# Layer 0's last turns: where the weighing's copies stand on ScalarE, and which PSUM tiles the last output chunks use

## The chip, the cores and the metric

The kernel runs on one core of a Trainium2 chip. The metric is the device time of one execution in microseconds (us), of which several are taken. A core has a matrix engine (TensorE, PE in the profile; its weight loads are a row of their own, PEld), a vector engine (VectorE, DVE), a scalar engine (ScalarE, ACT), GpSimd (POOL) and SyncE (SP), which here issues the DMAs. Each engine runs its own list of instructions in order, and they wait for one another through semaphores. All data is float32. Matrix products write to PSUM, which this kernel divides into eight banks of 128 partitions by 512 float32.

## The reference

The program is four residual layers on an image batch `x` of shape (2, 512, 64, 64): each layer normalises by groups of channels, computes a branch and adds it to `x`. The change lies in the first layer (attention over a 3x3 window and over pooled tokens at once, 8 heads of 64 channels) and at the first instructions of the second (attention with sampled keys). The first layer's branch, on the normalised tokens `xf` (N = 4096 pixels, C = 512), cut to what matters:

```python
q = (xf @ W_q + b_q).reshape(B, N, nh, hd).transpose(0, 2, 1, 3)
q_norm = _l2norm(q)
q_scaled = (q_norm + query_embedding[None]) * softplus(temperature)[None]
# k_local, v_local: the 9 shifted copies of normalised k, and of v
attn_local = jnp.einsum('bhnd,bhndk->bhnk', q_scaled, k_local)
# k_pool, v_pool: keys and values of 256 pooled tokens
attn_pool = jnp.einsum('bhnd,bhpd->bhnp', q_scaled, _l2norm(k_pool))
attn = softmax(concatenate([attn_local, attn_pool], axis=-1), axis=-1)
a_local, a_pool = (attn[..., :ll], attn[..., ll:])
lt = jnp.einsum('bhnd,hdk->bhnk', q_norm, learnable_tokens) + learnable_bias[None] + a_local
x_local = jnp.einsum('bhnk,bhndk->bhnd', lt, v_local)
x_pool = jnp.einsum('bhnp,bhpd->bhnd', a_pool, v_pool)
xo = (x_local + x_pool).transpose(0, 2, 1, 3).reshape(B, N, C)
out = (xo @ W_proj + b_proj).reshape(B, C, H, W)
```

The last line reshapes without a transpose, so a product of `xo` with `W_proj` gives rows of tokens that are added to the image in strides of eight (the `r` below). The second layer begins with the query `q = w_q x` of its normalised input, and with offsets of the sampled keys that come from a small network on strided pixels of that query.

## The kernel before

The two images of the batch are computed one after the other, so that everything here happens twice in an execution. The first layer (class `Local`) cuts an image into 16 units: four chunks of 128 channels times four quarters of 1024 pixels. A software pipeline of turns i = -4 to 16 runs over them (`run`, L2031 to L2060). In one turn several generators are stepped in rotation by `in_turn`: the normalisation and the projections of q, k and v for units three and four ahead, the products of unit i+1, the attention of unit i, the weighing of unit i-1.

- `learned` (L2412) computes the learnable part of the local weights: eight small products (L2419) and one activation (L2422), and then the scaled query (L2424).
- `tap_products` (L2436) copies a unit's query from SBUF to a query tile in PSUM, two halves (L2441, ACT), and DVE multiplies it by the nine shifted keys (L2447). `tap_sums` sums these products over the channels of a head on PE (L2474) into a tap bank.
- `attend` (L2486) takes the pooled scores (L2499, PE), exponentials (L2503, ACT), values (L2509, PE), their copy (L2511, ACT), the sums of the exponentials (L2525 and L2528, PE), the reciprocals on DVE, and sends the finished weights to DRAM (L2566).
- `weigh` (L2586) has ten steps for a unit. A DMA has spread a tap's row of weights over 64 partitions (L2584, from `rows`). ACT copies the tap's two halves to two PSUM banks (L2600). DVE multiplies them by the shifted values (L2608), or, in step 0, the unit's pooled output by the reciprocal sums (L2605). POOL adds the result to the unit's output (L2613). The next tap is fetched into the freed slot, of which there are three, or five for the last unit. The finished unit is stored to DRAM (L2619).
- `output` (L2211) multiplies the stored units by `W_proj`. `output(c4)` makes the image's channel chunk c4, in eight groups r of four products `product(ps, kc, r)` (L2227), one for each of the four chunks of contracted channels. `added` then runs three operations on DVE: the bias (L2231), the addition to the image (L2232) and the statistics for the next normalisation (L2233). After eight groups they are aggregated (L2303). `output(0)` runs in turn 14, `output(1)` in 15, `output(2)` in 16 and `output(3)` after the loop. Each reads the units through DRAM, but for `output(2)` and `output(3)` the unit of the last contracted chunk is read where the weighing leaves it (`late` in the profile).

The next layer's input is normalised by folding: from the statistics of a chunk come mean and reciprocal deviation (`part_stats`, `stats_in_steps`: PE L965, DVE L966 to L968, PE L970, ACT L971, DVE L972, POOL L973), `scale_part` (L978) scales the next layer's weights, and `thin` (L1208, ACT) copies strided pixels for the offsets.

The eight PSUM banks at this place are five of a ring (`bank()`, pool name `mm`), one tap bank (`tap`, pool `ppt`), and one query tile of two banks (`qs`, pool `pps`). A new tile in a place waits until the readers of the old one have ended. Two halves of one query tile are one tile in this accounting.

The order of PE's instructions is written by hand (`manual_schedule`) in the steady turns (3 to 11) and in turn 16. In turns 12 to 15 and in `output(3)` the scheduler of the framework orders them, as it orders the other engines everywhere. `issue_after(x)` tells it to place what stands inside behind the instruction x on their engine.

The second layer begins in `query_and_sample` (L1249): the offset network's first products go to four banks of the ring (L985), their sums to an accumulator `acc` of four banks (L992, L1006), which is read by L994 and L1009, then follow the activation of the offsets (L1223) and the query's first product (L134), whose result is read by L1264.

Of the kernel before, what the change touches and what calls it, by code (L numbers as in the profile page):

```python
# [9 lines left out]
F32 = mybir.dt.float32  # L10
# [6 lines left out]
P = 128  # L17
# [4 lines left out]
TB = 512  # L22
# [28 lines left out]
def in_turn(*gens):  # L51


    gens = list(gens)
    while gens:
        gens = [g for g in gens if next(g, gens) is not gens]
# [877 lines left out]
class Net(General):  # L934
# [314 lines left out]
    def query_and_sample(self, X, Y, wq, bq, grid, feats, top, wp, pp, ppk):  # L1249
# [9 lines left out]

        def query(blk):  # L1260
            for cc in range(KC):
                ps = pp.tile([P, TB], F32, name="mm")
                self.project(ps, wq[:, :, cc * P:(cc + 1) * P], X, blk)
                nc.scalar.activation(Y[:, cc, blk * TB:(blk + 1) * TB], ps, AF.Identity,  # L1264
                                     bias=bq[:, cc:cc + 1])
                yield
            nc.vector.tensor_reduce(top[:, :, blk], Y[:, :, blk * TB:(blk + 1) * TB], AX.X, ALU.max,
                                    apply_absolute_value=True)
# [673 lines left out]
class Local:  # L1942
# [77 lines left out]
    def run(self):  # L2020


        self.nmean = self.net.stats[:, 0]
        xs = self.pooled_tokens()
        heads = self.pooled_heads(xs)
        units = KC * self.UN
        unit = lambda u: u if 0 <= u < units else None
        self.pending = []
        for i in "qkv":
            self.fetch(i, 0)  # L2030
        for i in range(-4, units + 1):  # L2031
            k, q, ahead, u, before = (unit(i + n) for n in (4, 3, 1, 0, -1))
            self.steady = self.UN <= i + 1 and i < units - 4
            streams, ended = [], []
            stages = [self.norms(streams, ended)]
            if ahead is not None:
                stages.append(self.tap_products(ahead))
            if u is not None:
                stages.append(self.attend(u))
            if i == units:  # L2040
                stages.append(self.output(KC - 2))
            if before is not None:
                stages.append(self.weigh(before))
            if ahead is not None:
                stages.append(self.tap_sums(ahead))
            values = ([ahead] if i >= self.UN - 1 and ahead is not None
                      else {-4: [0], -3: [1, 2], -2: [3]}.get(i, []))
            stages.append(self.projections(k, q, values, streams))
            stages.append(self.normed(ended))
            if i < -2:  # L2050
                stages.append(islice(heads, 12 if i == -4 else None))
            if i == units - 3:
                stages.append(self.fetch_output())
            if units - 3 < i < units:
                stages.append(self.output(i - units + 2))
            if self.steady or i == units:
                with self.net.tc.manual_schedule(engines={mybir.EngineType.PE}):
                    in_turn(*stages)
            else:
                in_turn(*stages)  # L2060

        self.nc.sync.dma_start(self.next_w, self.d["w_q1"].rearrange("(kc p) o -> p kc o", p=P))
        in_turn(self.output(KC - 1))

# [144 lines left out]
    def output(self, c4):  # L2211
# [15 lines left out]
            nc.tensor.matmul(ps, toks[kc].rearrange("p (i r) -> p r i", r=8)[:, r, :], self.sq[kc],  # L2227
                             start=(kc == 0), stop=(kc == KC - 1))

        def added(ps, r):  # L2230
            nc.vector.tensor_tensor(ps, ps, self.pb, ALU.add)  # L2231
            nc.vector.tensor_tensor(xx[:, r], xx[:, r], ps, ALU.add)  # L2232
            nc.vector.bn_stats(st[:, r, :], xx[:, r])  # L2233

        def wide():
            qs = self.pps.tile([P, self.UT], F32, name="qs")
            return [qs[:, j * TB:(j + 1) * TB] for j in range(2)]

        def extras(r):
            if c4 and r == 2:  # L2240
                net.part_stats(slice(c4 - 1, c4), self.pp)
                net.thin(self.X, self.Y, c4 - 1)
            if c4 == KC - 1 and r:
                net.scale_part(self.next_w, slice(r // 2 - 1, r // 2))

        if c4 < KC - 2:
            yield
            yield
            for r in range(0, 8, 2):
                banks = [self.bank() for _ in range(2)]  # L2250
                for kc in range(KC):
                    for i, ps in enumerate(banks):
                        product(ps, kc, r + i)
                    if kc % 2:
                        yield
                for i, ps in enumerate(banks):
                    added(ps, r + i)
                extras(r)
        elif c4 < KC - 1:
            banks = wide() + [self.bank() for _ in range(2)]  # L2260
            for kc in range(KC - 1):
                for r, ps in enumerate(banks):
                    product(ps, kc, r)
                yield
            for r, ps in enumerate(banks):
                product(ps, KC - 1, r)
                added(ps, r)
            yield
            moments = net.stats_in_steps(slice(c4 - 1, c4), self.bank())
            for r, more in ((4, wide), (6, lambda: [self.bank() for _ in range(2)])):  # L2270
                banks = more()
                for kc in range(KC):
                    for i, ps in enumerate(banks):
                        product(ps, kc, r + i)
                    yield
                for i, ps in enumerate(banks):
                    added(ps, r + i)
                next(moments, None)
            net.thin(self.X, self.Y, c4 - 1)
        else:  # L2280
            banks = wide() + [self.bank() for _ in range(2)]
            for kc in range(KC - 1):
# [1 line left out]
                    product(ps, kc, r)  # L2284
            for r in (6, 7):
                nc.gpsimd.tensor_tensor(xx[:, r], xx[:, r], self.pb, ALU.add)
            for r, ps in enumerate(banks):
                product(ps, KC - 1, r)
                added(ps, r)
            extras(2)  # L2290
            for r in (4, 5):
                ps = self.bank()
                for kc in range(KC):
                    product(ps, kc, r)
                added(ps, r)
            extras(4)
            for r, ps in zip((6, 7), wide()):
                for kc in range(KC):
                    product(ps, kc, r)
                nc.vector.tensor_tensor(xx[:, r], xx[:, r], ps, ALU.add)  # L2300
                nc.vector.bn_stats(st[:, r, :], xx[:, r])
            extras(6)
        nc.vector.bn_aggr(net.mv[:, c4, :], st.rearrange("p b s -> p (b s)"))  # L2303
        yield

# [106 lines left out]
    def learned(self, u):  # L2412
# [6 lines left out]
                nc.tensor.matmul(ps[32 * q:32 * q + 32, :], self.tok[:, cc, :],  # L2419
                                 qn[:, j * TB:(j + 1) * TB], start=True, stop=True)  # L2420
        lt = self.lts()
        nc.scalar.activation(lt, ps, AF.Identity, bias=self.vec[:, V_LBR + cc:V_LBR + cc + 1])  # L2422
        self.lt[u] = lt
        nc.scalar.activation(self.qs[u % 3], qn, AF.Identity, bias=self.qb[:, cc:cc + 1],  # L2424
                             scale=self.sp_scale[:, cc:cc + 1])
# [60 lines left out]
    def attend(self, u):  # L2486
# [9 lines left out]
        def exponentials(j, k2):  # L2496
# [3 lines left out]
                                 qs[c, j * TB:(j + 1) * TB], start=True, stop=True)  # L2500
            prob[j, k2] = [self.prob() for _ in range(2)]
            for h in range(2):
                nc.scalar.activation(prob[j, k2][h], pS[h], AF.Exp)  # L2503

        def values(j):
            psO = self.bank()
# [79 lines left out]
    def weigh(self, u):  # L2586
# [7 lines left out]
        for i in range(10):  # L2594
# [1 line left out]
            parts = [t[:, j * TB:(j + 1) * TB] for j in range(2)]  # L2596

            banks = [self.bank() for _ in range(2)]
            for ps, part in zip(banks, parts):
                nc.scalar.copy(ps, part)  # L2600
            dy, dx = divmod(i - 1, 3)
            for j, (ps, part) in enumerate(zip(banks, parts)):
                if i == 0:
# [206 lines left out]
```

## Time and profile before

| what | us |
|---|---|
| three runs | 5073.88, 5074.23, 5079.57 |
| median | 5074.23 |
| the profiled execution | 5069.52 |
| its span, first to last instruction | 5067.7 |
| PE's work by the page | 4822.0 |

The page gives a row of busy time by engine. It then cuts the span into forty slices, and counts the groups of instructions with the same line, engine and operand names; for example, the copies of the weighing and the residual's products:

| group | count | us each |
|---|---|---|
| L2613, POOL addition of 128x1024 | nine a unit | 2.37 |
| L2227, PE product of 128x512 in two records | 32 an `output` | 0.86 |
| L2600, ACT copy of 128x512 | 20 a unit | 0.59 alone, 0.52 in a row |
| L2231, L2232, L2233, DVE 128x512 | 24 an `output` | 0.60 in a row |

In the timeline a line is a row of like instructions: its start, its length, engine, line, operation, the program's names of output and inputs, the shape, the count, and in brackets how long the engine was idle before and what ended that. A wait is written as the waiting instruction, `<-`, and the instruction that released it. The window's rows give each engine's busy time and the granted clock of PE as a share of full speed.

The places in the first batch: turn 14 begins at some 864 us, `output(0)` at 883, `output(2)` at 967, `output(3)` at 1002, the first query's product at 1044.

### The profile page before, as it was taken

What the parts mean: (1) busy time and instruction counts of PE and PEld (TensorE: products, weight loads), DVE (VectorE), ACT (ScalarE), POOL (GpSimd) and SP (SyncE); (2) the same over time, 40 slices, a digit from 0 to 9 for tenths busy, and PEclk for the clock granted to TensorE, in tenths of its full rate; (3) what the DMA queues carried; (4) which work ended last, traced back from release to release, by engine and by line L of the source; (5) the groups of instructions that cost most, each with busy time, mean ns of one, the idle gap of its engine ahead of it and who ended that gap; (6) DMA issues with size and microseconds to landing.
All of it is one profiled execution on the core that took longest, in us unless ns stands there. A gap on an engine that the chain in (4) does not pass through costs nothing. (4 is left out here: it accounts for less than half of the span.)

```text
span 5067.7 us, 48015 instructions
## 1 busy us (share of the span) xinstructions
PE 4822.0 (95%) x17027; PEld 1989.3 (39%) x17027; DVE 3069.5 (61%) x4010; ACT 1818.0 (36%) x3479; POOL 1848.2 (36%) x1218
## 2 busy tenths in 40 slices
PE   7999999999999999999999999999999999999998
PEld 3423332554334444433344233335543344444333
DVE  4266777754679533477732677777536794334776
ACT  1245555334323233321112555552443232333221
POOL 0035666501320145454500456664013201454554
PEclk9999999999999999999999999999999999999999
DMA  3035556600000000211110355565000000000111
GB/s 152 3 82 141 149 146 176 166 19 10 1 3 14 2 1 1 71 55 46 63 65 3 96 139 150 147 178 148 19 10 1 17 1 1 1 1 24 40 45 44
DMA packets 124172, 307.72 MB, mean 61 GB/s; under 512 B 20818, under 2 KB 33618, under 8 KB 122388
## 3 DMA queue, kind: packets, MB, share of 16 engines
q1 hardware_dynamic: 123924, 304.58, 20.8%
q8 instruction: 136, 2.23, 0.2%
q14 instruction: 112, 0.92, 0.1%
HBM read 256.01 MB, written 48.50 MB: 60 GB/s over the span
## 5 line engine op out<-in xcount | busy, mean ns | idle before, releaser
L134 PE MATMUL mm<-big,w 128*128 128x512 f32 x2496 | 1179.5, 616 | 32.3 <-DVE big L2404 9.5
L134 PEld LDWEIGHTS mm<-big,w 128*128 128x128 f32 x2496 | 458.5, 193 | 716.9 <-issue 558.8
L2613 POOL TENSOR_TENSOR late<-late,big 128x1024 f32<-128x1024 f32 x194 | 459.9, 2371 | 228.8 <-DVE big L2608 199.9
L2447 DVE TENSOR_TENSOR prods<-qs,big 128x1024 f32<-128x1024 f32 (+1 forms) x216 | 335.4, 1570 | 66.4 <-PE tap L2474 56.2
L1643 POOL TENSOR_TENSOR big<-big 128x512 f32<-128x512 f32 x224 | 277.6, 1272 | 219.3 <-ACT big L1634 219.3
L2608 DVE TENSOR_TENSOR big<-big,mm 128x512 f32<-128x512 f32 x388 | 254.6, 681 | 114.7 <-ACT mm L2600 113.3
L2600 ACT COPY mm<-big 128x512 f32<-128x512 f32 x432 | 247.4, 596 | 123.7 <-DMA big<-rows 78.2
L1634 ACT ACTIVATE big<-mm,ed 128x256 f32<-128x256 f32 x512 | 193.6, 489 | 233.1 <-DVE top L1630 200.4
L2518 POOL TENSOR_TENSOR late<-late 128x512 f32<-128x512 f32 x92 | 115.4, 1275 | 439.2 <-ACT late L2503 415.3
L2613 POOL TENSOR_TENSOR late<-late,tap 128x1024 f32<-128x1024 f32 x94 | 221.9, 2361 | 106.5 <-DVE tap L2608 93.6
L1446 POOL TENSOR_TENSOR wq<-prob 128x512 f32<-128x512 f32 x48 | 70.8, 1497 | 501.9 <-ACT prob L1443 501.9
L1898 PE MATMUL mm<-k,w 128*128 128x512 f32 x512 | 238.4, 609 | 12.3 <-DVE k L1891 7.3
L1630 DVE TENSOR_REDUCE top<-mm 128x1 f32<-128x512 f32 x256 | 159.0, 683 | 148.2 <-PE mm L1561 148.2
L1608 PE MATMUL mm<-w,big 128*128 128x512 f32 x512 | 235.3, 603 | 0.0
L134 PE MATMUL mm<-big,wq 128*128 128x512 f32 x512 | 232.4, 603 | 2.7 <-ACT off_t L1223 2.7
L1195 PE MATMUL mm<-big,wo 128*128 128x512 f32 x512 | 234.7, 604 | 0.0
L1356 PE MATMUL acc<-big,diag 128*128 128x512 f32 x512 | 227.3, 601 | 4.6 <-ACT diag L1361 4.6
L973 POOL TENSOR_TENSOR group_stats<-group_stats,cst 128x1 f32<-128x1 f32 (+1 forms) x20 | 12.1, 621 | 560.3 <-DVE group_stats L972 500.1
L1888 DVE RECIPROCAL psD<-psD 128x512 f32<-128x512 f32 x64 | 215.1, 3361 | 1.9
L134 PE MATMUL mm<-big,big 128*128 128x512 f32 x464 | 201.7, 594 | 0.5 <-DVE b_sr L1011 0.5
L2474 PE MATMUL tap<-prods,cst 128*32 128x512 f32 x1152 | 193.1, 604 | 4.8 <-DVE prods L2447 4.3
L1443 ACT ACTIVATE prob<-mm 128x512 f32<-128x512 f32 x256 | 133.0, 603 | 171.4 <-PE mm L1440 171.1
(419 smaller groups left out, 8152.4 us busy)
## 6 DMA issues: line engine op xcount, KB each, us to landing
big<-rows SPq DMA_DIRECT2D x432, 256.0 KB, 4.2
tap<-rows SPq DMA_DIRECT2D x208, 256.0 KB, 4.1
yd<-late SPq DMA_DIRECT2D x32, 512.0 KB, 3.0
lost_all<-lost SPq DMA_DIRECT2D x128, 128.0 KB, 3.0
out<-big SPq DMA_DIRECT2D x64, 256.0 KB, 2.0
big<-in_W_kv SPq DMA_DIRECT2D x8, 1024.0 KB, 10.1
rows<-late SPq DMA_DIRECT2D x64, 128.0 KB, 3.3
big<-in_x SPq DMA_DIRECT2D x32, 256.0 KB, 3.8
```

Of the source, the lines that this page charges most:

```text
L134: self.nc.tensor.matmul(ps, w[:, kc, :], X[:, kc, blk * TB:(blk + 1) * TB], start=(kc == 0), stop=(kc == KC - 1))
L1195: nc.tensor.matmul(ps, w[:, kc, oc * P:(oc + 1) * P], att[:, kc, :], start=(kc == 0), stop=(kc == KC - 1))
L1356: nc.tensor.matmul(accs[b], dg, src[:, b * TB:(b + 1) * TB], start=(j == 0), stop=(j == 6))
L1608: nc.tensor.matmul(ps, X[:, kc, lo:lo + P], wv[:, kc, :], start=(kc == 0), stop=(kc == KC - 1))
L1634: nc.scalar.activation(f[:, t, :], pS[h][i][:, t % 2, :], AF.Exp, bias=ed[:, t, 2 * cc + h:2 * cc + h + 1])
L1643: nc.gpsimd.tensor_tensor(a, a, part, ALU.add)
L1888: nc.vector.reciprocal(psD, psD)
L1898: nc.tensor.matmul(ps, self.wo[:, kc, oc * P:(oc + 1) * P], qs[:, kc, :], start=(kc == 0), stop=(kc == KC - 1))
L2447: self.nc.vector.tensor_tensor(self.pair(u, k)[:, :n].rearrange("p k (y x) -> p k y x", x=W), bcast(qs.rearrange("p (y x) -> p y x", x=W), ...
L2600: nc.scalar.copy(ps, part)
L2608: nc.vector.tensor_tensor(part.rearrange("p (y x) -> p y x", x=W), self.vx[:, y:y + self.UY // 2, dx:dx + W], ps.rearrange("p (y x) -> p y ...
L2613: nc.gpsimd.tensor_tensor(out, out, t, ALU.add)
```

## The change

It has four parts. (a) The copies of the weighing in turns 12 to 15 are placed on ACT behind the last activation of `learned` or the last exponential issued before them in the program. (b) `output(2)` runs the last products of its first four groups in two pairs, each followed by that pair's three DVE operations; the other four groups go one to the tap bank, two to the query tile and one to the tap bank, and the statistics of chunk 1 are no longer taken there. (c) `output(3)` has PE's order written by hand, works in the same pairs, takes the statistics of chunks 1 and 2 together between its groups, and uses the tap bank, a ring bank, half a query tile and the tap bank for its last four groups. (d) The query's very first product goes to the fourth bank of the accumulator.

```diff
@@ query_and_sample
-                ps = pp.tile([P, TB], F32, name="mm")
+                ps = acc[:, KC - 1] if not blk + cc else pp.tile([P, TB], F32, name="mm")
@@ run
+            self.units_left = units - i
...
-        in_turn(self.output(KC - 1))
+        with self.net.tc.manual_schedule(engines={mybir.EngineType.PE}):
+            in_turn(self.output(KC - 1))
@@ output
-        def added(ps, r):
-            nc.vector.tensor_tensor(ps, ps, self.pb, ALU.add)
+        def added(ps, r, bias=True):
+            if bias:
+                nc.vector.tensor_tensor(ps, ps, self.pb, ALU.add)
...
-        def extras(r):
-            if c4 and r == 2:
-                net.part_stats(slice(c4 - 1, c4), self.pp)
-                net.thin(self.X, self.Y, c4 - 1)
-            if c4 == KC - 1 and r:
-                net.scale_part(self.next_w, slice(r // 2 - 1, r // 2))
+        def single():
+            return self.ppt.tile([P, TB], F32, name="tap")
+
+        def group(ps, r, bias=True):
+            for kc in range(KC):
+                product(ps, kc, r)
+            added(ps, r, bias)
...
-                extras(r)
+                if c4 and r == 2:
+                    net.part_stats(slice(0, 1), self.pp)
+                    net.thin(self.X, self.Y, 0)
         elif c4 < KC - 1:
...
-            for r, ps in enumerate(banks):
-                product(ps, KC - 1, r)
-                added(ps, r)
-            yield
-            moments = net.stats_in_steps(slice(c4 - 1, c4), self.bank())
-            for r, more in ((4, wide), (6, lambda: [self.bank() for _ in range(2)])):
-                banks = more()
+            for r in (0, 2):
+                for i in (r, r + 1):
+                    product(banks[i], KC - 1, i)
+                for i in (r, r + 1):
+                    added(banks[i], i)
+            yield
+            group(single(), 4)
+            yield
+            pair = wide()
+            for i, ps in enumerate(pair):
                 for kc in range(KC):
-                    for i, ps in enumerate(banks):
-                        product(ps, kc, r + i)
-                    yield
-                for i, ps in enumerate(banks):
-                    added(ps, r + i)
-                next(moments, None)
+                    product(ps, kc, 5 + i)
+                yield
+            for i, ps in enumerate(pair):
+                added(ps, 5 + i)
             net.thin(self.X, self.Y, c4 - 1)
+            group(single(), 7)
         else:
...
-            for r, ps in enumerate(banks):
-                product(ps, KC - 1, r)
-                added(ps, r)
-            extras(2)
-            for r in (4, 5):
-                ps = self.bank()
-                for kc in range(KC):
-                    product(ps, kc, r)
-                added(ps, r)
-            extras(4)
-            for r, ps in zip((6, 7), wide()):
-                for kc in range(KC):
-                    product(ps, kc, r)
-                nc.vector.tensor_tensor(xx[:, r], xx[:, r], ps, ALU.add)
-                nc.vector.bn_stats(st[:, r, :], xx[:, r])
-            extras(6)
+            for r in (0, 2):
+                for i in (r, r + 1):
+                    product(banks[i], KC - 1, i)
+                for i in (r, r + 1):
+                    added(banks[i], i)
+            moments = net.stats_in_steps(slice(1, KC - 1), self.bank())
+            next(moments)
+            group(single(), 4)
+            next(moments, None)
+            net.thin(self.X, self.Y, KC - 2)
+            net.scale_part(self.next_w, slice(0, 1))
+            group(self.bank(), 5)
+            net.scale_part(self.next_w, slice(1, KC - 1))
+            group(wide()[0], 6, False)
+            group(single(), 7, False)
@@ learned
         lt = self.lts()
-        nc.scalar.activation(lt, ps, AF.Identity, bias=self.vec[:, V_LBR + cc:V_LBR + cc + 1])
+        self.ahead_of_copies = nc.scalar.activation(
+            lt, ps, AF.Identity, bias=self.vec[:, V_LBR + cc:V_LBR + cc + 1]).ins
@@ attend, exponentials
-                nc.scalar.activation(prob[j, k2][h], pS[h], AF.Exp)
+                self.ahead_of_copies = nc.scalar.activation(prob[j, k2][h], pS[h], AF.Exp).ins
@@ weigh
-            for ps, part in zip(banks, parts):
-                nc.scalar.copy(ps, part)
+            late = 0 < self.units_left < 5
+            with self.net.tc.issue_after(self.ahead_of_copies) if late else nullcontext():
+                for ps, part in zip(banks, parts):
+                    nc.scalar.copy(ps, part)
```

The aggregation in L2303 and the loops over the first three chunks of contracted channels stay as they were.

## The prediction

> **What bounds the kernel now.** I read the page's first part for the engine that the span hangs on, then TensorE's (PE's) waits over the changed stretch, then the granted clock there by windows, then each engine's timeline around each gap. The stretch runs twice, once per batch: 780 to 1060 us, and again some 2,525 us later. The page's shares:
>
> ```profile
> PE 4822.0 (95%) x17027; PEld 1989.3 (39%) x17027; DVE 3069.5 (61%) x4010; ACT 1818.0 (36%) x3479; POOL 1848.2 (36%) x1218
> ```
>
> PE is busy for 95%, so only its gaps and its half-clock time are to be had. The waits of PE from 780 to 1070 us (total, times, longest):
>
> ```profile
> PE mm L134 <- ACT late L2422: 4.1, 1, 4.1
> PE qs L2227 <- DVE big L2232: 3.0, 2, 2.6
> PE mm L2509 <- DVE late L2605: 2.9, 1, 2.9
> PE mm L2227 <- DVE big L2608: 2.6, 1, 2.6
> ...
> PE mm L134 <- ACT off_t L1223: 1.3, 1, 1.3
> ```
>
> Rows 1, 2, 4 and 5 are gaps that the diff touches: 4.1 (turn 14), 2.6 and 2.6 (turn 16), 1.3 (layer 1's start), 10.6 us per batch. Row 3 stays: L2509's operand hangs on tap data. The windows (length; busy and count of PE, PEld, DVE, ACT, POOL; granted clock):
>
> ```profile
> 860.00:880.00 20.00, 15.68 (x53) 4.24 (x48) 16.65 (x21) 7.77 (x14) 10.70 (x6) 0.83 0.73 202
> ...
> 980.00:1000.00 20.00, 16.98 (x36) 10.64 (x36) 18.40 (x31) 7.01 (x12) 14.46 (x7) 0.92 0.73 176
> ...
> 1040.00:1060.00 20.00, 17.92 (x66) 8.35 (x59) 5.01 (x14) 8.56 (x15) 0.00 (x0) 0.91 0.08 32
> ```
>
> The clock falls just where the gaps are. In 980 to 1000 DVE is busy for 18.40 of 20 us, so there PE's room ends soon at DVE.
>
> **The sum, part by part, per batch.** Lines are those of before.
>
> *Copies behind exponentials (turns 12 to 15).* No instruction is added; the two L2600 copies of a tap now stand on ACT behind the latest L2422 or L2503. At the turn-14 gap:
>
> ```profile
> 863.12 1.11 ACT L2600 COPY mm<-tap 128x512 f32<-128x512 f32 x2 [1.86 <-DMA tap<-rows]
> 864.17 0.68 ACT L2422 ACTIVATE late<-mm,vec 128x512 f32<-128x512 f32 x1
> 865.80 1.11 ACT L2600 COPY mm<-big 128x512 f32<-128x512 f32 x2 [0.95 <-DMA big<-rows]
> 866.84 0.58 ACT L2441 COPY qs<-big 128x512 f32<-128x512 f32 x1
> ```
>
> L2422, whose bank PE wants, stood behind copies that waited 1.86 us for a DMA. Now it and the second query copy L2441 come first: L2441's first half ends at 861.26, the second about 861.8, L2422 about 862.4. PE then goes on at about 863.2, as in its new order a tap sum that needs the first product of DVE comes ahead: 1.7 us sooner. What sets the turn's pace after that is DVE:
>
> ```profile
> 869.50 9.13 DVE L2447 TENSOR_TENSOR prods<-qs,big 128x1024 f32<-128x1024 f32 x8
> ```
>
> These eight (1.13 us each) fed PE's tap sums (872.42 to 878.60). One product runs early, in DVE's idle 2.84 us before 863.80; the rest begin near 868.1 and end about 877.2 instead of 880.96 (the ninth, at 879.75, ends there). L2227's first row moves from 883.43 to about 880: 2.6 to 3.4 us, I take 3.0. The half clock here (eight records of L134 take 6.53 us, against 3.67 in batch 1's query) lies beside DVE's products and gives no more. The copies end about 0.5 us later; cover is the slack of the weighing: its last POOL addition of unit 14 ends at 968.33 and PE reads it at 975.93, 7.6 us. SP: the loads of taps and stores are the same; one load of output(1) moves four issues earlier, 0.3 to 0.5 us of queue each, ahead of nothing late. In turns 12, 13 and 15 the copies' later place is covered in the same way (ACT is busy for 46.02 of the 80 us from 780): I take 0, with bounds of 0.7 us, about one exponential, gained or lost in each. Part: -3.0, bounds -3.4 - 2.1 = -5.5 and, if the products don't start sooner, +2.1.
>
> *Turn 16: pairs.* PE's second pair waited for L2232 of r0, since two halves are one tile; the last two banks for a weighing's L2608:
>
> ```profile
> 979.53 2.05 PE L2227 MATMUL qs<-sq,late 128*128 128x512 f32 x2 [2.57 <-DVE big L2232]
> ...
> 994.75 3.83 PE L2227 MATMUL mm<-sq,big 128*128 128x512 f32 x8 [2.55 <-DVE big L2608]
> ```
>
> Both gaps go, 5.12 us, as does the half clock between (four records at 981.37 took 2.83 us, 1.88 elsewhere). But DVE's order holds 40 operations of about 0.60 us from its first weighing product at 974.52 to the bias addition of r6: 974.5 + 24 = 998.5. PE, unhindered, ends r7 at 975.93 + 20 rows of 0.86 + about 0.8 (r5 waits for r1's additions in the query tile) = 993.9. The next product, output(3)'s first, wants the query tile that L2231 of r6 still reads: a new gap of about 4.5 us. It begins at 998.4, not 1001.99. Twelve rows later come the products with the last unit's output: 998.4 + 10.3 = 1008.7, or 1012.1 if the new gap drags two half-clock stretches of 1.7 us behind it, against 1012.49; POOL's last addition is no earlier than before:
>
> ```profile
> 1004.81 2.37 POOL L2613 TENSOR_TENSOR late<-late,tap 128x1024 f32<-128x1024 f32 x1
> ```
>
> I take the middle with one half-clock stretch, 1010.4: -2.1; bounds -3.8 and +1 (r5's wait 0.8, twice the half clock). Here the Trainium skill speaks against the change ("TensorE: Matmul & The Clock Gate", "What's actually happening"): the clock halves after an idle window of some 3.4 us in free-running windows. The trace agrees on the length, but halves after gaps of 2.57 and even 1.33 + 0.75 us. By the page only the new gap of 4.5 us could halve it, and if it covers no window the part would be -3.8; by the rows it does.
>
> *output(3).* One round of statistics fewer: two PE products and four small DVE operations, about 0.3 us of PE, and the 0.28 us before L965 at 1033.88. New: the joined round's second product L970 stands behind r4 on PE, its L968 behind r4's L2231 and the last normalisation statistics on DVE: some 3 operations of 0.6 = 1.7 us. Who waits is r5 and all behind. Part +1.1; bounds 0 (if L968 is done while r4's four rows, 3.4 us, run) and +3.4 (with a half clock).
>
> *First query in another bank.* The product waited for L1223 to read its bank; now for the copy out of the statistics' accumulator:
>
> ```profile
> 1042.38 0.16 DVE L1009 COPY bq<-acc 128x4 f32<-128x4 f32 x1 [5.02 <-PE acc L1006]
> ...
> 1043.61 5.37 PE L134 MATMUL mm<-big,wq 128*128 128x512 f32 x8 [1.33 <-ACT off_t L1223]
> ```
>
> 1043.61 against 1042.54 is -1.0. In batch 0 this product runs at half clock (5.37; batch 1 3.67); with 2.1 us of idle cut to about 1.1, I let it go: -1.7 there, 0 in batch 1. Bounds: 0 (copies of wq on POOL, last at 1037.43, later than that) and -1.3 -1.7.
>
> Sum: batch 0 -3.0 -2.1 +1.1 -1.0 -1.7 = -6.7; batch 1 -5.0, with 0.6 more for its larger gaps there (2.71 twice) and its second half-clock stretch: -5.6. Together -12.3. The profiled run took 5069.52 us (span 5067.7, 1.8 outside): 5057. The median of the runs is 4.7 us (0.09%) over it; on the median, 5074.23 - 12.3 = 5062.
>
> **The rivals.**
>
> *All the gaps go and no new wait comes.* For it: DVE has 3.48 us idle before 974.52 and could start sooner if turns 14 and 15 end sooner, and the new gap would shrink. Against: DVE at 18.40 of 20. Per batch 4.1 + 5.1 + 1.3 and half clocks of 1.7 twice + 2.7 = 16.6 us; both 33: 5041.
>
> *The gain stops at DVE and POOL.* The earlier turn 14 ends up in the new gap, since DVE and POOL set the late rows: the first -3.0 and the -2.1 become one -2.1 together, or nothing with two half clocks. Per batch -2.1 +1.1 -1.0 = -2 to +1, both -4 to +2: about 5072, within 0.2%. For it: POOL's last addition at 1007.18, only 5.3 us before its reader. Against: the chain of weighing starts sooner by what turn 14 gains.
>
> *Slower: the copies hold up the weighing.* A copy queued behind an exponential waits for PE's scores (ACT L2503 waited 15.8 us for L2499 from 780 to 980, longest 4.7), and behind it wait L2608 on DVE, L2613 on POOL, the free slot and the next tap's load. One such 4.7 us hold in each of four turns is 18.8; it decides from 7.6 us, the slack of unit 14. 18.8 - 7.6 - 3.8 of other gains (2.1 + 1.0 + 1.7 - 1.1, batch 0) = +7.4 per batch: 5089. Against: DVE's waits for copies there (20.0, 11.1 and 6.0 us, 28 in all) come mostly behind loads, and ACT is idle for half the time.
>
> *The change of ACT's order moves nothing*, since the order was so already. Possible for turns 12, 13 and 15; turn 14's lines above speak against it. Without that part: -2.1 +1.1 -1.0 -0.85 = -2.9 per batch, 5068; it is counted with the second rival.
>
> **How the numbers follow.** A measurement of this kernel tells about 0.2% (10 us) from no change: faster is below 5064.1, slower above 5084.4. Chances: forecast 0.5 (own range 5054 to 5069), all gaps gone 0.15, stops at DVE and POOL 0.23, copies hold up 0.12. Of the forecast's range the part over 5064 goes to no change: 0.5 x 0.15 = 0.07. Faster 0.43 + 0.15 = 0.58, same 0.30, slower 0.12. The range reaches down to halfway into the first rival and over the second: 5047 to 5077.
>
> **What would show it.** Right: in turn 14 L2422 ahead of the tap's copies and L2227's first row about 3 us sooner after the turn's start; no gap inside turn 16's four pairs over 1 us; a gap of 4 to 5 us at output(3)'s first query row, released by DVE L2231, with half clock after it; 1 to 2 us at the joined L970; the first query released by L1009. Wrong: the new gap missing (then the first rival), POOL's last addition of unit 14 or 15 later relative to its reader (then the third), or PE's busy time in 860 to 900 unchanged.

## The result, and the profile after

| | median, us | lowest to highest | runs |
|---|---|---|---|
| before | 5074.55 | 5068.96 to 5081.50 | 20 |
| changed | 5082.73 | 5073.08 to 5094.56 | 20 |

The changed kernel is slower: the ratio is 1.0014 (95% interval 1.0008 to 1.0020), some 7 us. That is within the 0.2% that the forecast called no change, but on the other side of zero than the forecast, clear of the measurement's own interval, and outside the range given.

The page's first part says little (busy us, share of the span and count by engine), as PE's share is what it was and the span is 7 us longer:

```profile
span 5074.7 us, 47985 instructions
...
PE 4826.0 (95%) x17019; PEld 1993.2 (39%) x17019; DVE 3062.9 (60%) x4002; ACT 1817.9 (36%) x3477; POOL 1847.6 (36%) x1216
```

PE's waits of the changed kernel over the first batch's stretch, 780 to 1080 us (total, times, longest):

```profile
PE mm L2517 <- DVE late L2615: 5.2, 2, 2.8
PE tap L2482 <- DVE prods L2455: 5.1, 3, 2.5
PE qs L2229 <- DVE big L2235: 5.1, 2, 4.4
PE mm L970 <- DVE group_stats L968: 2.9, 1, 2.9
...
PE acc L134 <- DVE bq L1009: 0.4, 1, 0.4
```

Three of the four old gaps are gone: the 4.1 us at L2422 (now L2429; its 0.6 us that are left stand in turn 13), the 2.6 us between the two pairs, the 2.6 us for the ring banks. The 1.3 us at the first query became 0.4. Three new waits stand in their place: for DVE's products at a tap sum (5.1 in three places, where it was 0.5), 4.4 us at output(3)'s first product, 2.9 us at L970. And a second wait of the values product for L2615 has joined the old one. Another wait of before is gone as well, of L134 in turn 13:

```profile
PE mm L134 <- DVE big L2608: 2.0, 2, 1.1
```

New gaps were taken for old ones of about the same sum.

Because a profile is one execution, I cut the stretch into stages by PE's own first instructions and compared stages over all kernels of this study that share them. From the start of one unit's exponential sums (L2525 before) to the next is turn 12, then 13; then to output(0)'s first product, and so on; the sums come at the end of a turn, so the stage up to output(0) begins at 856.88 us in before, some 7 us ahead of turn 14's own start. The last stage ends with the query's first product:

| stage, us per batch | before, batch 0 / 1 | changed, 0 / 1 | mean of 18 stretches without the hold | mean of 8 with it |
|---|---|---|---|---|
| turn 12 | 41.7 / 42.1 | 42.6 / 42.9 | 42.0 | 43.1 |
| turn 13 | 43.4 / 44.3 | 46.5 / 48.1 | 44.9 | 47.2 |
| to output(0) | 26.6 / 26.6 | 26.5 / 24.6 | 26.8 | 26.1 |
| output(0) | 37.8 / 37.8 | 38.5 / 37.8 | 37.8 | 38.1 |
| output(1) | 44.4 / 47.0 | 45.9 / 44.5 | 46.0 | 45.5 |
| output(2) | 36.4 / 37.4 | 33.1 / 33.9 | | |
| output(3) and the first query | 47.0 / 45.3 | 52.3 / 50.5 | | |

"The hold" is the copies' place behind the exponentials; the kernels with it in all four turns are the changed one, x2, x13 and x14, those without it before, x1, x3 to x7, x11 and x12. It costs turns 12 and 13 some 3.5 us and gives 0.7 back before output(0). output(2) gains 3.4 us, and output(3) loses 5.3 even with the query's gain in it.

### The profile page after: what moved, and what is told of

Read it like the earlier page. It is cut to its first block, busy times and chain, and to the rows that moved or that the text cites. A ratio compares the mean times of both kernels' runs of the same rounds, so it can differ in the third digit from the quotient of the medians.

```text
span 5074.7 us, 47985 instructions
## 1 busy us (share of the span) xinstructions
PE 4826.0 (95%) x17019; PEld 1993.2 (39%) x17019; DVE 3062.9 (60%) x4002; ACT 1817.9 (36%) x3477; POOL 1847.6 (36%) x1216
## 3 DMA queue, kind: packets, MB, share of 16 engines
q8 instruction: 136, 2.23, 0.2%
## 5 line engine op out<-in xcount | busy, mean ns | idle before, releaser
L134 PE MATMUL mm<-big,w 128*128 128x512 f32 x2496 | 1173.6, 614 | 21.1 <-DVE big L2411 9.4
L134 PEld LDWEIGHTS mm<-big,w 128*128 128x128 f32 x2496 | 457.7, 193 | 703.7 <-issue 558.1
L134 PE MATMUL mm<-big,wq 128*128 128x512 f32 x496 | 223.4, 599 | 0.0
L973 POOL TENSOR_TENSOR group_stats<-group_stats,cst 128x1 f32<-128x1 f32 (+2 forms) x18 | 11.3, 646 | 557.0 <-DVE group_stats L972 496.8
L134 PE MATMUL mm<-big,big 128*128 128x512 f32 x464 | 201.7, 595 | 0.5 <-DVE b_sr L1011 0.5
```

The costliest lines, as they stand in the source:

```text
L134: self.nc.tensor.matmul(ps, w[:, kc, :], X[:, kc, blk * TB:(blk + 1) * TB], start=(kc == 0), stop=(kc == KC - 1))
```

## The experiments

Ratios are to the kernel before on the same chip, with 95% intervals; 0.0010 is 5 us.

**The parts by themselves.** Four kernels: the changed one without the hold, and before with one part each.

```diff
# x1_no_hold, from the changed kernel
-            late = 0 < self.units_left < 5
+            late = False
```

x1_no_hold: 

> The changed kernel with the weighing's copies left where the scheduler puts them (no placing behind exponentials); all else as changed. Theory M (the loss is made in turns 12 to 15 by the copies' new place, some 6 us for both batches together, and in output(3) by the joined second product L970, some 7.7 us; output(2) gives 1.7 back and the first query 2): the time falls by about 6 us from the changed kernel, to 2 to 4 us above before, and the gap at L970 of some 2.8 us stays. Theory R1 (all of the loss is in output(3), the copies are harmless): it stays 8 us above before. Theory R2 (all of the loss is the copies'): it falls to 2 to 5 us below before.

x2_hold_only (before, with the three edits of `learned`, `exponentials` and `weigh`): 

> The kernel before with only the copies placed behind the exponentials in turns 12 to 15. Theory M: about 6 us above before; PE waits at a tap sum for DVE's products for some 2.1 us in turn 13 and 2.5 us in turn 14. Theory R1: no change, within 2 us. Theory R2: 8 to 12 us above before. The forecast on record would have 6 us below before.

x3_query_only (before, with the first line of the diff): 

> The kernel before with only the first query's bank taken from the accumulator. All theories: 1 to 3 us below before; the first product is released by L1009 after 0.4 us instead of by L1223 after 1.3 us, so 0.9 us per batch, and where the half clock behind it goes another 1.7 us.

x4_out2_only (before, with `output(2)`'s branch of the changed kernel, and `part_stats(slice(1, 3))` in output(3)): 

> The kernel before with only output(2) in pairs on the tap bank and the query tile; the statistics of chunk 1 go with those of chunk 2 at their old place in output(3). Theory M: output(2) ends some 8 us sooner by its own gaps, output(3) then waits some 4.4 us at its first product for L2235 of r6, with half clock behind it, and what is left is a gain of 1 to 2 us in all. The forecast on record would have 2.1 us per batch, 4 in all. A rival (the waits weigh more): 2 us or more above before.

| kernel | ratio | interval |
|---|---|---|
| x1_no_hold | 1.0009 | 1.0000 to 1.0018 |
| x2_hold_only | 1.0012 | 1.0003 to 1.0021 |
| x3_query_only | 0.9997 | 0.9988 to 1.0006 |
| x4_out2_only | 0.9997 | 0.9988 to 1.0006 |

The hold alone makes the kernel slower, against the forecast's 6 us of gain. Without it the rest is still not faster. So x2 speaks against R1 (no change) and x1 against R2 (2 to 5 us below before): the loss has two places. The query and output(2) move less, each by itself, than can be measured. The first rows of x2_hold_only's waits of PE from 780 to 950 us show what the hold does:

```profile
PE tap L2476 <- DVE prods L2449: 5.2, 3, 2.6
PE mm L2511 <- DVE late L2609: 4.9, 2, 2.8
PE mm L134 <- DVE tap L2612: 1.4, 1, 1.4
```

The first row is the scheduler: with the hold it puts tap sums forward on PE, in turn 13 ahead of the projections' L134, and there PE stands for 2.1 us until DVE has a product; before, L134 stood at this place for 1.13 and 0.87 us. The second row holds a new wait in turn 14, followed back below.

In x3_query_only's timeline of PE the first product now follows after 0.41 us and runs at full clock, 3.67 us where before's batch 0 took 5.37:

```profile
1043.34 1.05 PE L1006 MATMUL acc<-cst,hatx 128*128 128x1 f32 x8 [0.75 <-ACT hatx L994]
1044.81 3.67 PE L134 MATMUL acc<-big,wq 128*128 128x512 f32 x8 [0.41 <-DVE bq L1009]
```

**output(3), and its cure.**

x5_out3_only (before, with output(3)'s branch and PE's order by hand): 

> The kernel before with only output(3) changed (PE's order by hand, pairs, statistics between the groups; here those of chunk 2 alone, since output(2) still takes chunk 1's). Theory M: a gap of some 2.8 us at the second product L970 in each batch, with one or two half-clock stretches behind it (1.7 to 3 us), less 0.3 us at L965: 8 to 11 us above before. Rival R3 (output(3) costs only where output(2)'s pairs run ahead of DVE): within 3 us of before, with no gap at L970 over 1 us.

```diff
# x6_late_moments, from x1_no_hold
             group(single(), 4)
-            next(moments, None)
-            net.thin(self.X, self.Y, KC - 2)
             net.scale_part(self.next_w, slice(0, 1))
             group(self.bank(), 5)
+            next(moments, None)
+            net.thin(self.X, self.Y, KC - 2)
```

x6_late_moments: 

> x1_no_hold with one thing moved: the second half of the joined statistics round (L970) comes behind r5 instead of behind r4. Theory M: the gap of 2.85 us and the half clock behind it go, 4 to 5 us per batch: 8 to 10 us below x1_no_hold, so some 5069 to 5072 us where before is at 5075. Rival R3: no more than 2 us below x1_no_hold.

x5 came to 1.0016 (1.0007 to 1.0025), x6 to 0.9989 (0.9980 to 0.9998), 0.0020 (by the two intervals, within 0.0013) or some 10 us below x1_no_hold: theory M on both. In the changed kernel's timeline of PE:

```profile
1028.24 1.02 PE L2229 MATMUL tap<-sq,late 128*128 128x512 f32 x2
1032.12 0.58 PE L970 MATMUL mm<-group_stats,cst 128*128 128x2 f32 x2 [2.85 <-DVE group_stats L968]
1032.56 5.47 PE L2229 MATMUL mm<-sq,prods 128*128 128x512 f32 x6
```

and in its timeline of DVE:

```profile
1029.33 0.68 DVE L2234 TENSOR_TENSOR mm<-mm,kp 128x512 f32<-128x512 f32 x1
1029.91 0.15 DVE L966 TENSOR_TENSOR group_stats<-channels_mv,mm 128x2 f32<-128x2 f32 x1
1030.04 0.69 DVE L2235 TENSOR_TENSOR big<-big,mm 128x512 f32<-128x512 f32 x1
1030.65 0.15 DVE L967 TENSOR_TENSOR group_stats<-group_stats 128x2 f32<-128x2 f32 x1
1030.72 0.69 DVE L2234 TENSOR_TENSOR tap<-tap,kp 128x512 f32<-128x512 f32 x1
1031.32 0.68 DVE L2236 BATCH_NORM_STATS2 gn_st<-big 128x6 f32<-128x512 f32 x1
1031.92 0.14 DVE L968 TENSOR_TENSOR group_stats<-group_stats,channels_mv 128x2 f32<-128x2 f32 x1
```

r4's last product ends at 1029.26 us. DVE is then still behind with the group before it: that group's bias, addition and statistics and r4's own bias, four operations of 0.6 us, and two short ones stand ahead of L968, an operation of 0.14 us, without a pause between them. L970, the next instruction on PE after r4, waits for all of them. Behind the gap six records take 5.47 us, 2.74 in the next group (batch 0; in batch 1 the gap is as long and the clock stays full). In x6_late_moments DVE's order is the same, but while it gets to L968 PE runs r5, and L970 waits for nothing:

```profile
1024.38 2.74 PE L2229 MATMUL mm<-sq,prods 128*128 128x512 f32 x6
1026.96 1.02 PE L2229 MATMUL mm<-sq,late 128*128 128x512 f32 x2
1027.82 0.28 PE L970 MATMUL mm<-group_stats,cst 128*128 128x2 f32 x2
```

**The 4.4 us ahead of output(3).**

```diff
# x7_query_pair_first, from x6_late_moments
-            group(single(), 4)
-            yield
             pair = wide()
...
-                    product(ps, kc, 5 + i)
+                    product(ps, kc, 4 + i)
...
-                added(ps, 5 + i)
+                added(ps, 4 + i)
+            group(single(), 6)
+            yield
             net.thin(self.X, self.Y, c4 - 1)
-            group(single(), 7)
+            group(self.bank(), 7)
```

x7_query_pair_first: 

> x6_late_moments with another order of tiles in output(2): r4 and r5 in the query tile, r6 in the tap bank, r7 in a ring bank, so that output(3)'s first product waits for r5's additions instead of r6's. Theory M (the 4.36 us gap is the query tile behind DVE's order): the gap falls below 1.5 us and the half clock behind it goes; 2 to 4 us per batch below x6_late_moments, until POOL's last additions of the weighing bind. Rival R4 (DVE and POOL bind turn 16 whatever tile is used): the gap only moves, to r7's ring bank or to the products with the last unit's output, and the time is within 2 us of x6_late_moments.

```diff
# x11_bias_on_pool, from x6_late_moments
         elif c4 < KC - 1:
+            for r in range(8):
+                nc.gpsimd.tensor_tensor(xx[:, r], xx[:, r], self.pb, ALU.add)
...
-                    added(banks[i], i)
+                    added(banks[i], i, False)
...
-            group(single(), 4)
+            group(single(), 4, False)
...
-                added(ps, 5 + i)
+                added(ps, 5 + i, False)
...
-            group(single(), 7)
+            group(single(), 7, False)
```

x11_bias_on_pool: 

> x6_late_moments with output(2)'s eight bias additions moved from DVE to eight additions of 128x512 on POOL, made on the image before the products, in POOL's idle 10 us before its first addition of the last unit's weighing. Theory M (DVE's order sets the 4.36 us gap ahead of output(3)): eight operations of 0.6 us fewer on DVE, the gap falls below 1.5 us, 2 to 4 us per batch below x6_late_moments. Rival R4 (POOL's weighing binds): the gap falls but the additions of the last unit's weighing end as late or later, PE waits at the products with its output, and the time is within 2 us of x6_late_moments or above it.

x12_bias_on_pool_pair_first (x7 with the same edit): 

> x7_query_pair_first with the same move of output(2)'s bias additions to POOL. Theory M: the 4.1 to 4.4 us gap that moved to r4 falls below 2 us; 2 to 4 us per batch below x7_query_pair_first. Rival R4: within 2 us of x7_query_pair_first or above it.

| kernel | ratio | interval | output(2), us, batch 0 / 1 |
|---|---|---|---|
| x6_late_moments | 0.9989 | 0.9980 to 0.9998 | 33.1 / 33.6 |
| x7_query_pair_first | 0.9982 | 0.9973 to 0.9991 | 33.7 / 34.0 |
| x11_bias_on_pool | 0.9962 | 0.9949 to 0.9975 | 27.5 / 27.5 |
| x12_bias_on_pool_pair_first | 0.9965 | 0.9952 to 0.9978 | 28.0 / 28.9 |

Another order of tiles only moves the gap, as R4 had it (the two ratios differ by less than their intervals). x7's timeline of PE:

```profile
985.66 1.45 PE L2229 MATMUL mm<-sq,late 128*128 128x512 f32 x3
991.21 3.29 PE L2229 MATMUL qs<-sq,big 128*128 128x512 f32 x4 [4.10 <-DVE big L2235]
...
1006.88 1.88 PE L2229 MATMUL qs<-sq,prods 128*128 128x512 f32 x4
```

The gap ahead of output(3) (1006.88) is gone, and one of 4.10 us stands ahead of r4: in DVE's order the tile's last reader comes late wherever the tile is used. Taking eight operations off DVE removes the gap; the gain, 0.0027 or some 14 us for both batches, is more than the 4 to 8 us expected, and output(2) is 5.6 and 6.1 us shorter. The windows from 984 to 1004 us (length; busy and count of PE, PEld, DVE, ACT, POOL; clock; the last two figures are the DMA's), x6_late_moments first:

```profile
984.00:1004.00 20.00, 16.11 (x37) 10.88 (x35) 19.37 (x33) 7.97 (x14) 14.19 (x6) 1.00 0.86 205
```

and x11_bias_on_pool:

```profile
984.00:1004.00 20.00, 18.65 (x44) 13.20 (x43) 18.65 (x32) 9.88 (x19) 14.34 (x7) 1.00 0.89 217
```

DVE is full in both; PE does 2.5 us more in the second. All that is left in x11's waits of PE from 960 to 1050 us:

```profile
PE mm L2229 <- DVE big L2620: 1.3, 1, 1.3
PE acc L1006 <- ACT hatx L994: 0.8, 1, 0.8
PE acc L134 <- DVE bq L1009: 0.4, 1, 0.4
PE mm L985 <- DVE big L978: 0.4, 1, 0.4
```

My expectation had POOL make these additions in its idle 10 us ahead of the last unit's weighing. It did not: the scheduler set them far earlier, two of the eight from 754.0 us on and six between 797.5 and 875.9 us, and that idle 10 us is still there.

**Which part of the hold.** Before, with the hold in part.

```diff
# x8_hold_turn14: late = self.units_left == 2
# x10_hold_turn13: late = self.units_left == 3
# x9_hold_exps: late as in the change; `learned` no longer sets ahead_of_copies
```

x8_hold_turn14: 

> The kernel before with the copies placed behind the exponentials in turn 14 alone. Theory M (the hold costs in turns 12 and 13 and gains about 1 us per batch in turn 14): 1 to 4 us below before. Rival R5 (turn 14 with its new 2.5 us wait for DVE's first product loses too): 2 us or more above before.

x9_hold_exps: 

> The kernel before with the copies of turns 12 to 15 placed behind the exponentials alone, no longer behind the activation of `learned` as well. Theory M2 (the hold's loss is made in turns 12 and 13, where the scheduler moves tap sums forward on PE and they then wait for DVE's products; the earlier `learned` gains about 1 us at turn 14): the 4.1 us gap at turn 14's start is back, the 2.1 us wait at a tap sum in turn 13 stays, and the time is 6 to 9 us above before. Rival R6 (the loss comes from `learned`, whose place moves the tap sums): within 2 us of before.

x10_hold_turn13: 

> The kernel before with the hold in turn 13 alone, whose copies are those ahead of `learned` at the start of turn 14. Theory M2: the 4.1 us gap is replaced by some 2.5 us at a tap sum and turn 13 itself keeps its old order but for its end: about 1 us per batch gained, 1 to 4 us below before. Rival R7 (what PE gains at turn 14's start is lost to the new wait at the values product L2509, 2.1 to 2.4 us in the runs with the hold): within 2 us of before, or up to 4 above.

| kernel | ratio | interval | turn 13, us, batch 0 / 1 | gap at turn 14's start |
|---|---|---|---|---|
| x8_hold_turn14 | 1.0008 | 0.9999 to 1.0017 | 43.8 / 46.8 | 3.9 / 4.4 at L134 |
| x9_hold_exps | 1.0008 | 1.0000 to 1.0017 | 44.7 / 46.1 | 4.3 / 4.8 at L134 |
| x10_hold_turn13 | 1.0005 | 0.9996 to 1.0014 | 45.4 / 44.2 | 2.5 / 2.7 at a tap sum |

These three settle little about the total. x8's expectation was wrong in its premise: PE's order is that of before, and the old gap stays, since the copies ahead of `learned` belong to turn 13. x10 has the gap changed as expected but no gain with it, which is R7's side. x9 has what M2 named, the 4.1 us gap back and the 2.1 us wait at a tap sum still in turn 13, but its time is some 4 us above before, between M2's 6 to 9 and R6's 2. All three intervals touch or hold 1, so no single part of the hold can be called the one that costs, and why x8 came out at 1.0008 with the gaps of before stays open.

**Does the hold lose by itself?** It might have lost only because turn 16 could not use an earlier output(0). So it was tried on the kernel whose turn 16 is relieved, and the cure at L970 on the changed kernel.

x13_after_late_moments (the changed kernel with x6's edit): 

> The changed kernel itself, the hold on the copies kept, with only L970 moved behind r5. Theory M (two separate losses: the gap at L970 with its half clock, 8 to 11 us for both batches, and the hold, 2 to 6 us): 8 to 11 us below the changed kernel, so from 3 us below to 1 us above before. Rival R8 (the two losses share one cause, and what is saved at L970 is lost to the hold's later weighing): no more than 3 us below the changed kernel.

x14_best_with_hold (x11 with `late` as in the change): 

> x11_bias_on_pool with the copies placed behind the exponentials again in turns 12 to 15. Theory M (the hold costs by itself): 2 to 6 us above x11_bias_on_pool. Rival R9 (the hold's loss came only because DVE and POOL were late in turn 16, which this kernel has relieved): the same as x11_bias_on_pool or up to 6 us below, as the earlier start of output(0) now reaches the end.

x13: 1.0003 (0.9994 to 1.0012), against 1.0014 of the changed kernel, about 6 us less, by the two intervals within some 5: nearer to M's 8 to 11 than to R8's 3 at most, but it excludes neither. x14: 0.9981 (0.9972 to 0.9990) against x11's 0.9962 (0.9949 to 0.9975): the hold costs 0.0019 (by the intervals, within 0.0016) or some 10 us by the ratios, 7.5 by the medians (5066.49 against 5058.96). R9 falls: the hold costs where turn 16 is relieved as well. The first two rows of x14's waits of PE from 780 to 950 us are those of x2; the third, at the end of turn 12, is 0.6 us at most in the other kernels with the hold:

```profile
PE tap L2484 <- DVE prods L2457: 5.3, 3, 2.8
PE mm L2519 <- DVE late L2617: 5.2, 2, 2.8
PE mm L2535 <- DVE tap L2620: 1.9, 1, 1.9
```

x11_bias_on_pool beats both kernels: 0.9962 of before, some 19 us.

## Why the prediction was wrong

**Copies behind exponentials: the step that failed.** I wrote that L2227's first row "moves from 883.43 to about 880: 2.6 to 3.4 us, I take 3.0", and for turns 12, 13 and 15 "I take 0". With the hold, turns 12 and 13 are 1.2 and 2.3 us longer, and output(0) follows only 0.7 us sooner: a loss of some 2.6 us per batch (from turn 12 to the end of output(1), with a standard error of 0.9 from the spread of the stretches), where a gain of 3.0 was forecast and 2.1 was the upper bound. Two things were left out.

First, turn 13 was given no working. I looked for what the hold does at the gap that the profile showed, not at the same instructions one turn earlier. There the order on PE changes as well. In before's timeline of PE:

```profile
819.79 3.70 PE L134 MATMUL mm<-big,w 128*128 128x512 f32 x8 [1.13 <-DVE big L2608]
824.36 3.70 PE L134 MATMUL mm<-big,w 128*128 128x512 f32 x8 [0.87 <-DVE big L2608]
```

and in the changed kernel's:

```profile
824.97 1.05 PE L2482 MATMUL tap<-prods,cst 128*32 128x512 f32 x4 [2.10 <-DVE prods L2455]
826.67 8.82 PE L134 MATMUL mm<-big,w 128*128 128x512 f32 x16 [0.64 <-ACT late L2429]
```

The new wait stands where two old ones of 2.0 us together stood, so it is no loss of 2.1 us. Over all its waits PE stood for 4.5 us of turn 13 with the hold (mean of the 8 stretches) and for 3.8 without (of the 18), but the granted clock was at half for 6.3 us against 2.4. So 0.7 of the 2.3 us are waits; the rest fits the half clock, which costs up to half of its own length. x9_hold_exps speaks for this: it has the same 2.1 us wait, with half clock of 0 and 3.4 us, and its turn 13 took 44.7 and 46.1 us, against a mean of 44.9 without the hold. Over turns 12 to 14 together the half clock is no longer than without the hold (8.2 us against 8.3): it moved from the stage up to output(0), where 1.4 us are left of 5.7 and where I had seen it lie beside DVE's products, to turn 13. Why it moved is not shown, and turn 12's 1.2 us were not traced.

Second, at turn 14 the start went as forecast. PE stood for 2.5 us at a tap sum instead of 4.1 at L2422. The gain was lost before output(0), at the values product. In the changed kernel's timeline of POOL in batch 0:

```profile
877.45 1.28 POOL L2294 TENSOR_TENSOR big<-big,kp 128x512 f32<-128x512 f32 x1 [0.98 <-PE mm L134]
878.69 2.38 POOL L2623 TENSOR_TENSOR late<-late,big 128x1024 f32<-128x1024 f32 x1
```

of SP's queue:

```profile
874.28 1.11 SPq L2574 DMA_DIRECT2D rows<-late  x2
881.09 0.33 SPq L2629 DMA_DIRECT2D yd<-late  x1
881.52 1.27 SPq L2592 DMA_DIRECT2D big<-rows  x2
```

of ACT:

```profile
887.39 1.11 ACT L2610 COPY mm<-big 128x512 f32<-128x512 f32 x2 [7.79 <-DMA big<-rows]
```

and of PE:

```profile
888.76 1.94 PE L2517 MATMUL mm<-late,vp 128*64 128x512 f32 x8 [2.41 <-DVE late L2615]
```

With the weighing a little later, a bias addition of output(3) that waits for PE (L2294) now stands on POOL ahead of the unit's last tap; before, it stood behind. So the unit ends at 881.07. SP has the store of that unit (L2629) ahead of the next unit's first tap loads (L2592). From the rows' own store to these loads it took 7.2 us; before, 2.9 (869.61 to 872.48). The copies wait 7.79 us for the loads, DVE multiplies, and only then is the ring's bank free for PE.

All eight stretches with the hold show the same chain. The rows' store comes 9.5 to 10.9 us after the start of the stage, against 12.4 to 13.2 without the hold; but the unit's store ahead of the loads still comes only at 15.2 to 17.9 us, the values product waits 0.37 to 2.77 us, and output(0) begins 9.4 to 10.1 us behind that store in each of them. Where the store is earliest, in batch 1 of the changed kernel (15.2), the wait is 0.37 us and output(0) comes 1.9 us sooner than before; where it is latest, in x14 (17.9), whose POOL has x11's additions as well, output(0) comes later than in x11.

I named SP's queue for one load that moves, and took the weighing's slack as the 7.6 us between unit 14's end and its use in output(2). The nearer reader was the next unit's tap loads, behind the store in the same queue, with no slack.

**output(3): right mechanism, wrong size.** The new stall at the joined L970 was named and priced at 1.7 us, part +1.1 in all, with 3.4 as the bound with half clock. It measured 2.85 in both batches (3.4 in x5), and in batch 0 the next group's rows took some 2.7 us longer behind it, at half clock. The cure was worth about 5 us per batch (x6 against x1, 10 us for both). What the sum left out is that DVE was still at work on the group before r4: four operations of 0.6 us stood ahead of L968 where I had counted three operations in all. The half clock stood in my bound, not in my sum.

**Turn 16: right.** The forecast was a new gap of "about 4.5 us" released by DVE and some 0.8 us at r5; measured 4.36 in both batches, and 0.73 and 1.4. In x4, which has this part alone, the stages from output(2) to the first query are together 2.2 and 2.0 us shorter than before's; the forecast was 2.1. In the changed kernel the half clock at output(3)'s first rows (3.81 and 2.99 us for four records each, 1.88 elsewhere) takes 3.0 of the 3.4 us back that output(2) gains. The rule of the Trainium skill that was weighed there ("TensorE: Matmul & The Clock Gate", "What's actually happening") has an idle window of about 3.4 us halve the clock. The gap of 4.36 us was followed by 6.83 us of half clock in both batches. In batch 0 it filled 3.37 of the 3.41 us ahead of the half clock, as by the rule; in batch 1 only 2.26, and gaps of 2.1 and 2.85 us did so too, which the rule alone would not have.

**The first query: right.** -1.0 forecast, 0.9 measured in the wait (1.33 to 0.41), and the half clock went in the changed kernel's batch 0. In batch 1 it came, so the 1.7 us was luck where it was right and is no sure gain.

**The sum and the rivals.** By the measured parts, per batch: the hold +2.6, output(2) -3.4, output(3) with the query +5.3, together +4.5, or 9 us for both; the runs say 7 to 8. The third rival had part of the cause, that the hold delays the weighing, but a price of 15 us and a wrong point from which it decides (unit 14's slack of 7.6 us); its other gains add up to 3.7, not 3.8. The parts' own upper bounds, +2.1, +1, +3.4 and 0, add up to +6.5 us per batch or 5087, above what was measured. The range failed since its upper end, 5077, was drawn over the second rival and left out the slower one, as if not both the hold and output(3) could go to their bounds; both did.

## What to carry to other kernels

When an instruction is made to wait on one engine, follow the stores and loads that hang on it through the DMA queue's own order: the first thing late may be another unit's load behind a store, not the reader for which slack was counted. And give every turn that an edit covers the same working as the one where the gap is seen. If a scheduler orders the engines, compare its new order on the bounding engine row by row, and look at what a new wait replaces before it is called a loss.

A gap that was released by an engine busy for 19 of 20 us did not go away with another buffer; it moved (x6 to x7). Taking work off that engine, eight additions to one with idle time, is what removed it.

Where a short operation of a chain (L968) stands in a full engine's order, what waits for it waits for all that is ahead of it there, of earlier groups too. Here the engine that needed its result had other work to run meanwhile, and one group later L970 was free.

## What the runs showed of the hardware

The granted clock fell to half for 3.41 us behind gaps well below that length: in the changed kernel behind 2.10 and 0.64 us in turn 13 (at 826.70), 2.54 us (871.07) and 2.83 us (935.92). It stayed there for 6.83 us behind 4.36 us, in both batches. Whether a given gap does it changes from batch to batch: 2.85 us at L970 brought 6.83 us of half clock in batch 0 and none in batch 1, and 0.75 and 0.41 us at the first query brought 3.41 us only in batch 1. Where it begins is not free: in each of the profiles of before, the changed kernel, x2, x6 and x11 all half-clock stretches start on one grid of 3.413 us, within 0.01 us. At L970 the gap of batch 0 lay with 2.23 us in one step of the grid (65%), and the half clock followed; that of batch 1 was cut into 1.68 and 1.18 us (49% and 34%), and none followed. The idle share does not decide alone, as the step ahead of the first query's half clock was idle for 34% only.

Over the whole profile the half clock came to 168 us in before and 178 in the changed kernel.
